# A tuned three-layer cross network on one core: eight 32-row loads near the end, and the first pairs' x-products inside one group of small matmuls

## The chip, the cores and the metric

The kernel runs on one core of one Trainium2 chip. The metric is the device time of the launch in microseconds. A core has a tensor engine (PE, with its weight loads listed as PEld), a vector engine (DVE), a scalar engine (ACT), GpSimd (POOL) and a queue engine (SP) that issues most of the transfers between main memory (HBM) and on-chip memory (SBUF). PE writes into PSUM, a small memory of eight banks of 128 x 512 floats. Each engine runs its own instructions strictly in the order in which they were written; between engines they wait on semaphores.

## The reference, cut to what matters

Three layers cross the input with itself, and the result is one number for each of the 1024 batch rows. `x` has the shape (1024, 64, 16): batch, features, embedding.

```python
for i in range(3):
    z = einsum('bfe,bge->bfge', x0, h)              # every feature of x by every row of h
    y = einsum('oc,bce->boe', Ws[i], z) + bs[i]     # 128 outputs
    x_i, h = (y[:, :64], y[:, 64:]) if i < 2 else (y, y)
    xs.append(x_i)
pooled = sum(concatenate(xs, axis=1), axis=2)
return pooled @ fc_w.T + fc_b
```

All arithmetic is in float32.

## The kernel before, in words

**Tiling.** The batch is cut into 32 chunks of 32 rows, so that a chunk of `x` is a matrix of 64 features by 512 columns (32 rows by 16 embedding places). Only the rows of W0 that feed the next layer are contracted chunk by chunk; everything behind the final `fc` is folded into a few vectors and small matrices at the start. For a chunk the kernel forms blocks `z` (128 x 2048: four 128 x 512 matrices side by side) as an elementwise product of two shifted copies of the chunk, `xa` (128 x 2048) and `xb` (128 x 512, four of them, j = 0 to 3). PE contracts these blocks with `w_all`, 64 output columns at a time, and two such matmuls run side by side in the two halves of the array. Chunks 0, 1, 4 and 5 (pairs 0 and 2) are done plainly in the banks `acc`. From pair 3 on, two chunks are done together, with sums of blocks (`ws`) that save one of eight contractions; their banks are called `alpha`, `beta`, `delta` and `gamma`. There are thirteen such pairs (`NPAIR`, pairs 3 to 15). Chunks 2 and 3 (pair 1) come last and end in the banks `q`.

**The small matmuls.** Three kinds of product have fewer than 128 rows. `along_x` and `v0x` multiply the chunk's 64 rows of x (`xx`, or `xs`, which is the same pair of chunks with its halves exchanged) by the 64 x 64 matrices `v1` and `v0`; the result of `v0x` is the bank `y`, which DVE then multiplies by x (`x_v0x`, line 353) and sums (`sums`, line 356). `far` multiplies 32 rows of `d` by `dq`, `dh` or `dqh`. `d` holds products of features that lie 32 apart: `far_bank` (line 221) copies the loaded rows to PSUM on ACT, `far_product` (line 225) multiplies them on DVE. In the profile all of these matmuls, and the large ones, have line 598, since one helper (`mm`) records them; they are told apart by their tiles. `plain_extras` (line 652) is the group of small matmuls for chunks 0, 1, 4 and 5; `joint_extras` that of two later pairs; `end_extras` (line 1072) the last one.

**What sets the order.** From line 586 on, nothing is issued at once: `at(when, fn, ...)` puts a call on a list, which is sorted by `when` at line 1160 and then issued. One unit of `when` is about one step of two neighbouring matmuls. `T0 = 33` is the start of pair 3's window, `SPAN = 31` the length of a window. A call's place on the list sets its place in the queue of its engine, and the sequence in which scratch blocks (`take`, `used`) and PSUM banks (`bank`) are handed out.

**Scratch and banks.** The blocks `z` come from a list of 14. PSUM banks have roles: `turns["acc"]` holds four, `turns["set"]` two and `turns["y"]` two, each used in rotation. `pair_bank` (line 683) fixes, at the first pair, which of them serve as `even` (two), `three` (three) and `odd` (one). The `y` banks also hold the PSUM copies of `xb` that `second` (line 625) makes on ACT ahead of a DVE product: with two banks in rotation, a copy waits until DVE has read the copy before the last.

**Around the first window.** `weigh` (line 607) multiplies two 128 x 2048 weight blocks on POOL, `add_up` (line 611) sums each on DVE, and `place` (line 616) writes each sum with four small ACT instructions into `v0` (for v = 0) and `v1` (for v = 1). `v0x` for pairs 0 and 2 needs `v0`, `plain_extras` needs `v1`. `factors` (line 340) takes a finished plain chunk out of its bank: an ACT copy (line 344) and one or two DVE products (lines 348, 349, 351). The first two banks of `y` become pair 3's `alpha` and `delta`.

**Near the end.** `load_last_d` (line 199) loads for pair 1 the rows from which `d` is made (`ds`, tile d) and a second factor (`xds`, tile xs). SP then issues `load_turned` (line 186) and `load_xx` (line 182) for the same pair. DVE runs `far_product` for pair 1 directly ahead of `w_hb` of the last of the thirteen pairs (line 778), which takes a bank out that the first matmul of `end_extras` writes again. Each SP transfer uses one of eight semaphores in rotation, so that a transfer's issue waits for the landing of the eighth transfer before it.

Of the kernel before, what the change touches and what calls it, by code (L numbers as in the profile page):

```python
# [45 lines left out]
CB = 32  # L46
N = CB * E
# [6 lines left out]
XR = 128 + NI  # L54
# [15 lines left out]
def cin_kernel(ctx, tc, xra, xrb, wh, w0r, w1h, w2t, wx1, wx0, vec, lin, out):  # L70
# [7 lines left out]
    halves = [slice(0, F), slice(F, 128)]  # L78

    turns = {"acc": [0, 1, 2, 3], "set": [4, 5], "y": [6, 7]}  # L80
# [40 lines left out]
    fcb, fcr = vs[:, 3:4], vs[:, 68:196]  # L121
# [9 lines left out]
    for base in (0, 64, -64):  # L131
        nc.gpsimd.affine_select(
            out=shift, in_=shift, compare_op=ALU.not_equal, fill=1.0, base=base,
# [43 lines left out]
    def pair_tile(kept, name, k):  # L177
        if k not in kept:
            kept[k] = sp.tile([128, N], F32, tag=name, name=f"{name}_{k}")
        return kept[k]  # L180
# [17 lines left out]

    def load_last_d():
        for kept, name, first in ((ds, "d", 32), (xds, "xs", 0)):  # L200
            for h in halves:
                nc.sync.dma_start(
                    out=pair_tile(kept, name, 1)[h],
                    in_=bass.AP(
                        tensor=xra.tensor, offset=(2 * XR + first) * N,
                        ap=[[XR * N, 2], [N, 32], [1, N]],
                    ),
                )

    def copy_x(c):  # L210
# [18 lines left out]
    def far_pair(when, k):  # L229
        at(when - 2.6, far_bank, k)  # L230
        at(when, far_product, k)
# [50 lines left out]
    acc = const_tile("acc", [128, 2, NCH // 2, CB])  # L282
# [147 lines left out]
    for h in range(2):  # L430
        at = slice(32 * h, 32 * h + 32)
# [156 lines left out]
    def at(when, fn, *args, **flags):  # L588
        ops.append((when, len(ops), fn, args, flags))
# [91 lines left out]
    ROLES = {}  # L681

    def pair_bank(p, name):
        if name not in p:
            n = (p["k"] - 3) % 2
            if not ROLES:
                ROLES["even"] = [turns["acc"][m] for m in (0, 1)]
                ROLES["three"] = [turns["acc"][2], *turns["set"]]
                ROLES["odd"] = turns["acc"][3]
            c = (p["k"] - 3) // 2  # L690
            if name == "delta":
                where = ROLES["odd"] if n else ROLES["even"][1]
            elif name == "alpha":
                where = ROLES["three"][c % 3] if n else ROLES["even"][0]
            else:
                where = ROLES["three"][(c + 1 + n) % 3]
            p[name] = bank(f"{name}_{p['k']}", where)
        return p[name]
# [98 lines left out]
    def make_pair(t, p, when, mixed):  # L797
        a, b = p["a"], p["b"]
        for when, c, j, name, uses in (
            (when[0], b, 2, "B22", 5), (when[1], b, 0, None, 0), (when[2], b, 0, "T3", 9),  # L800
            (when[3], a, 0, "X", 5), (when[4], b, 3, "B22", 5), (when[5], b, 1, None, 0),
            (when[6], b, 1, "T3", 9), (when[7], a, 1, "X", 13 if p["k"] > 3 else 5), (when[8], a, 2, "B21", 5),
            (when[9], a, 3, "B21", 5),
        ):
            if name is None:
                at(t + when, w_both, p, j)
                continue
            if name == "B21" and j == 2 and p["k"] == 3:
                at(t + when, w_product, p, c, j, name, uses, engine=nc.gpsimd)
                continue  # L810
            if name != "T3":
                ahead = 3.3 if p["k"] > 4 and name == "B22" and j == 2 else 2.7
                if p["k"] == 3 and name == "X" and j == 1:
                    ahead = 9.1
                at(t + when - ahead, second, c, j)
            at(t + when, w_product, p, c, j, name, uses)
        t2, t1, t4 = ("T2", "X", "T3"), ("T3", "B22", "T2"), ("T2", "T2", "B21")
        for when, j, names in zip(
            mixed, (0, 1, 1, 0, 1, 1, 0), (t2, (*t2, 0, 2), (*t2, 2), t1, t1, t4, t4)
        ):  # L820
            if names == t4 and j and p["k"] % 2:
                at(t + when - 1.5, w_mix, p, j, *names, 0, 2)
                names = (*t4, 2)
            at(t + when, w_mix, p, j, *names)
        at(t + 29, lambda: used(p["B21"][p["k"] % 2 ^ 1]))
# [81 lines left out]
    def load_pair(t, p, b0, a0, b1, a1):  # L907
        a, b = p["a"], p["b"]
        at(t + b0, load_xa, b)
        at(t + b0, load_xb, b, 2, 0)  # L910
        at(t + a0, load_xa, a)
        at(t + a0, load_xb, a, 0)
        at(t + b1, load_xb, b, 3, 1)
        at(t + a1, load_xb, a, 1, 2, 3)
        early = p["k"] > 3
        at(t - 8 if early else t + 1, load_d, p["k"])
        far_pair(t + (6.9 if p["late"] else 17.5), p["k"])
        at(t + 1.1, load_xx, p["k"])


# [31 lines left out]
    for when, c in ((-7, 4), (1, 5)):  # L952
        at(when, copy_x, c)
        at(when, copy_d, c)
    for v, fc, mul, add, put in ((0, fcr[:, 0:64], 4, 16.6, 16.7), (1, fcr[:, 64:128], 5, 20, 20.1)):
        at(mul, weigh, v, fc)
        at(add, add_up, v)
        at(put, place, v, v1 if v else v0, QS if v else 1.0)
# [3 lines left out]
        at(when, product, c, j, engine=nc.gpsimd, uses=NI)  # L962
    for k in (0, 2):
        at(-0.6, new_y, k, "acc")
        at(24.5, x_v0x, k, k // 2)
        at(24.6, sums, k, slice(0, 128), slice(1, 2), slice(0, CB), slice(k // 2, k // 2 + 1))
    for c in (4, 5):
        at(-0.5, new_acc, c)
    contract_all(0, 4, start=True)
# [1 line left out]
        at(16 + t, contract, 5, t // NI, t % NI, True)  # L971
    for k, when in ((0, 6), (2, 12)):
        far_pair(when, k)
    at(24.1, v0x, 0)
    at(24.1, v0x, 2)
    at(29.1, plain_extras)
    for c in (0, 1):
        at(34.5, factors, c)
    at(34.6, sums, 0, slice(0, 128), slice(0, 1))
    for c, when in ((4, 12.7), (5, 21.4)):  # L980
        at(T0 + when, factors, c)
    at(T0 + 29.1, sums, 2, slice(0, 128), slice(0, 1))

# [9 lines left out]
    for n, p in enumerate(pairs):  # L993
        t = T0 + SPAN * n
        q, after = pairs[n - 1], pairs[n + 1] if n + 1 < NPAIR else None
        if n == 0:
            load_pair(t, p, -39.9, -33.3, -39.8, -27)
            make_pair(
                t, p, (-23.4, -20.7, -20.4, -16.5, -17.2, -16.8, -15.8, -7, -13.5, 3),
                (-14, -6.9, -6.8, 7.2, 12.4, 17.6, 15.9),  # L1000
            )
            first_window(
                t, p, after, [[(contract_half, 5, 3, i, h) for i in (1, 2, 3)] for h in range(2)]
            )
        else:
            load_pair(t, p, -34, -28, -27.8, -27.7)
            make_pair(
                t, p, (-21.4, -18.7, -18.4, -15.8, -12.2, -9.5, -6.1, -6.2 if n % 2 else -2, 1.6, 4.2),
                (-5, 1.6, 3.6, 7.2 if n % 2 else 0.2, 12.4, 18.6, 18.5 if n % 2 else 16.9),
            )  # L1010
            (a_leads if n % 2 else o_leads)(t, p, q, after)
            if n % 2:
                end_pair(t, q, (0.7, 21.4, 21.5, 21.3, 36))
            else:
                end_pair(t, q, (0.7, 22.3, 22.4, 9.9, 36))
# [236 lines left out]
```

## Time and profile before

| | |
|---|---|
| median of 3 runs | 442.82 us (441.85 to 443.77) |
| the profiled execution | 442.79 us, of which 440.9 us are the span from its first to its last instruction |
| granted TensorE clock | 1.0 throughout |
| DVE, POOL, ACT busy | 389.2, 378.0, 114.1 us |
| transfers | 102.04 MB, 231 GB/s on average |

The profile is one execution on the chip. A row of the timeline gives start, duration, engine, line, operation and `out<-in` by the program's names without buffer numbers; what stands in brackets is the time in which the engine sat idle before it and what ended that. Each float32 matmul leaves two rows, so that x8 is four matmuls. Where two of them run side by side in the array, both have the same start. A row of the chain of waits names what the end of the program was waiting for at that time. "SPq" is the issue of a transfer, "DMA" its time until landing.

### The profile page before, as it was taken

What the parts mean: (1) busy time and instruction counts of PE and PEld (TensorE: products, weight loads), DVE (VectorE), ACT (ScalarE), POOL (GpSimd) and SP (SyncE); (2) the same over time, 40 slices, a digit from 0 to 9 for tenths busy, and PEclk for the clock granted to TensorE, in tenths of its full rate; (3) what the DMA queues carried; (4) which work ended last, traced back from release to release, by engine and by line L of the source; (5) the groups of instructions that cost most, each with busy time, mean ns of one, the idle gap of its engine ahead of it and who ended that gap; (6) DMA issues with size and microseconds to landing.
All of it is one profiled execution on the core that took longest, in us unless ns stands there. A gap on an engine that the chain in (4) does not pass through costs nothing.

```text
span 440.9 us, 6152 instructions
## 1 busy us (share of the span) xinstructions
PE 435.3 (99%) x2296; PEld 154.9 (35%) x2296; DVE 389.2 (88%) x288; ACT 114.1 (26%) x210; POOL 378.0 (86%) x143
## 2 busy tenths in 40 slices
PE   9999999999999999999999999999999999999987
PEld 6333343334333333333333333333333333333335
DVE  4897799999998999989998989989999889986754
ACT  3153361323311222121322213212221213213111
POOL 5828898899998989899898989989898998989900
PEclk9999999999999999999999999999999999999999
DMA  7997997199649972899729984599818997397400
GB/s 275 411 384 184 352 411 314 46 325 241 224 132 312 325 220 84 229 326 273 247 85 250 341 239 159 155 322 307 225 67 250 335 248 240 119 234 247 113 4 3
DMA packets 36567, 102.04 MB, mean 231 GB/s; under 512 B 6741, under 2 KB 7541, under 8 KB 30073
## 3 DMA queue, kind: packets, MB, share of 16 engines
q1 hardware_dynamic: 33128, 86.84, 58.1%
q0 software_dynamic: 1872, 13.63, 14.9%
q10 hardware_dynamic: 1536, 1.18, 1.0%
q8 instruction: 18, 0.29, 0.3%
q14 instruction: 13, 0.10, 0.1%
HBM read 86.36 MB, written 1.64 MB: 200 GB/s over the span
## 4 chain that ended last, share of the span: by engine, by line
PE 71%; DMA 18%; DVE 6%; issue 3%; SPq 2%; ACT 1%; ACTq 0%; DVEq 0%
PE alpha L598 45%; PE delta L598 20%; DMA xa<-in_xra 6%; DMA xs<-in_xra 4%; DMA z<-in_w2t 3%; PE q L598 2%; DVE z L740 2%; PE acc L598 2%; DVE z L293 2%; DMA xb<-in_xrb 2%; PE y L598 1%; DMA md<-z 1%; DMA z<-md 1%; DMA z<-in_w0r 1%; DVE shift L613 1%
## 5 line engine op out<-in xcount | busy, mean ns | idle before, releaser
L757 POOL TENSOR_TENSOR z<-z,z 128x2048 f32<-128x2048 f32 (+1 forms) x85 | 301.9, 3608 | 21.3 <-PE delta L598 11.1
L740 DVE TENSOR_TENSOR z<-xa,xp 128x2048 f32<-128x2048 f32 x103 | 231.6, 2281 | 10.4 <-ACT xp L627 8.5
L598 PE MATMUL alpha<-z,ws 128*64 128x512 f32 x616 | 228.5, 593 | 0.0
L598 PE MATMUL alpha<-z,w_all 128*64 128x512 f32 x416 | 183.5, 593 | 0.0
L598 PEld LDWEIGHTS alpha<-z,ws 128*64 128x64 f32 x616 | 71.7, 137 | 83.1 <-issue 82.7
L598 PE MATMUL delta<-z,w_all 128*64 128x512 f32 x208 | 95.5, 592 | 0.0
L598 PE MATMUL delta<-z,ws 128*64 128x512 f32 x208 | 91.4, 592 | 0.0
L627 ACT COPY xp<-xb 128x512 f32<-128x512 f32 x88 | 51.1, 587 | 117.6 <-DVE z L740 96.6
L598 PEld LDWEIGHTS alpha<-z,w_all 128*64 128x64 f32 x416 | 56.4, 137 | 58.7 <-issue 58.1
L293 DVE TENSOR_TENSOR z<-xa,xp 128x2048 f32<-128x2048 f32 (+2 forms) x29 | 43.3, 1546 | 8.0 <-ACT xp L627 7.3
L598 PEld LDWEIGHTS delta<-z,ws 128*64 128x64 f32 x208 | 28.4, 137 | 32.5 <-issue 31.7
L598 PEld LDWEIGHTS delta<-z,w_all 128*64 128x64 f32 x208 | 28.4, 137 | 30.9 <-issue 30.5
L293 POOL TENSOR_TENSOR z<-xa,xb 128x2048 f32<-128x2048 f32 x6 | 27.5, 4639 | 10.9 <-DMA xb<-in_xrb 10.9
L598 PE MATMUL acc<-z,w_all 128*64 128x512 f32 x128 | 28.2, 593 | 0.0
L301 PE MATMUL acc<-z,w_all 128*64 128x512 f32 x96 | 21.5, 596 | 0.1
L358 DVE TENSOR_REDUCE acc<-uu 128x64 f32<-128x1024 f32 (+2 forms) x19 | 19.6, 1035 | 0.2
L746 DVE TENSOR_TENSOR xp<-xp,xb 128x512 f32<-128x512 f32 x26 | 18.1, 695 | 0.5
L293 POOL TENSOR_TENSOR z<-xa,xb_gps 128x512 f32<-128x512 f32 (+1 forms) x6 | 14.1, 2376 | 5.2 <-ACT xb_gps L372 4.5
L774 ACT COPY snap<-delta 64x512 f32<-64x512 f32 x13 | 7.6, 581 | 41.1 <-PE alpha L598 36.2
L771 ACT ACTIVATE snap<-alpha,vs 64x512 f32<-64x512 f32 x13 | 8.9, 684 | 35.4 <-PE alpha L598 35.3
L598 PEld LDWEIGHTS acc<-z,w_all 128*64 128x64 f32 x128 | 10.6, 137 | 17.1 <-issue 16.5
L768 ACT COPY alpha<-alpha 64x512 f32<-64x512 f32 x13 | 7.3, 558 | 34.1 <-PE alpha L598 21.0
(137 smaller groups left out, 341.5 us busy)
## 6 DMA issues: line engine op xcount, KB each, us to landing
xa<-in_xra SPq DMA_DIRECT2D x32, 1024.0 KB, 9.0
xb<-in_xrb SPq DMA_DIRECT2D x128, 256.0 KB, 7.8
z<-z POOLq DMA_DIRECT2D x13, 1024.0 KB, 11.3
d<-in_xra SPq DMA_DIRECT2D x28, 128.0 KB, 5.6
xx<-in_xra SPq DMA_DIRECT2D x28, 128.0 KB, 11.5
z<-in_w2t SPq DMA_DIRECT2D x2, 1024.0 KB
z<-in_wx SPq DMA_DIRECT2D x2, 1024.0 KB, 9.8
xs<-in_xra SPq DMA_DIRECT2D x16, 128.0 KB, 6.4
```

What stands on the lines that cost most here:

```text
L293: engine.tensor_tensor(blocks[zs[c, j]][:, at, :], xas[c][:, at, :], xbs[c][j].unsqueeze(1).to_broadcast([128, last - first, N]), ALU.mult,)
L301: nc.tensor.matmul(accs[c][halves[i % 2]], w_all[:, j * NI + i, 0:64], blocks[zs[c, j]][:, i, :], start=(j == 0 and i < 2), stop=(j == las ...
L358: nc.vector.tensor_reduce(acc[rows, of, k, half], uu[rows, of if at is None else at, E * half.start : E * half.stop].rearrange("p k (b e) ...
L598: nc.tensor.matmul(out, w, rhs, start=start, stop=stop, skip_group_check=True)
L613: nc.vector.tensor_reduce(shift[:, 32 * v : 32 * v + 32], w, AX.X, ALU.add)
L627: nc.scalar.copy(out, xbs[c][j])
L740: engine.tensor_tensor(blocks[b], xas[c], xbs[c][j].unsqueeze(1).to_broadcast([128, NI, N]), ALU.mult)
L746: nc.vector.tensor_tensor(bank, bank, xbs[p["b"]][j], ALU.add)
L757: nc.gpsimd.tensor_tensor(*(blocks[b][:, first:last] for b in (o, x, y)), ALU.subtract if in1 == "T3" else ALU.add,)
L768: nc.scalar.copy(beta(p), alpha(p))
L771: nc.scalar.activation(p["t"][p["O"]], alpha(p), AF.Identity, bias=bh1[p["A"]])
L774: nc.scalar.copy(p["hs"][p["A"]], delta(p))
```

## The change

**Eight transfers for four.** `load_last_d` read each half of d and of xs (64 rows) with one transfer whose source pattern has two outer steps (two chunks) of 32 rows. It now issues eight transfers of 32 plain rows, in the order d, d, d, d, xs, xs, xs, xs, all on SP and ahead of the same `load_turned` and `load_xx`.

**The first pairs' x-products.** `v0x` for pairs 0 and 2 moves on the list from 24.1 to 27.1, and `plain_extras` from 29.1 to 27.1, so that the sixteen small matmuls stand together: PE now runs all but one step of chunk 5's plain contraction first, then `v0x` (four matmuls), then `along_x` (four) and `far` (eight), then the one step left, then pair 3's window. `add_up` and `place` for v = 1 move from 20 to 16.7, directly behind those for v = 0. The products of `y` with x (`x_v0x`) go from 24.5 to 27.5, their `sums` from 24.6 to 27.9.

**What gives way.** On DVE the product of pair 3's block for b, j = 1 (tile z, from xp_3) now stands behind the second `add_up` instead of between the two, and the two `sums` of pairs 0 and 2 stand behind pair 3's product "X", j = 1, instead of ahead of it. On ACT the copy for that product "X" stands behind the second `place` instead of ahead of it. `factors` of chunk 4 moves from 12.7 to 15.5 (one DVE product later), pair 3's `far_pair` from 17.5 to 27 (on DVE behind three more 128 x 2048 products, on ACT behind two more copies). `ROLES["three"]` lists the same three banks in another order, so that pair 4's `alpha` takes a bank of chunk 0 instead of one of chunk 4.

No matmul is added or removed, POOL's order is unchanged, and SP has four instructions more.

```diff
     def load_last_d():
         for kept, name, first in ((ds, "d", 32), (xds, "xs", 0)):
-            for h in halves:
+            for m in range(4):
                 nc.sync.dma_start(
-                    out=pair_tile(kept, name, 1)[h],
-                    in_=bass.AP(
-                        tensor=xra.tensor, offset=(2 * XR + first) * N,
-                        ap=[[XR * N, 2], [N, 32], [1, N]],
-                    ),
+                    out=pair_tile(kept, name, 1)[32 * m : 32 * m + 32],
+                    in_=xra[2 + m % 2, first : first + 32],
                 )
...
-                ROLES["three"] = [turns["acc"][2], *turns["set"]]
+                ROLES["three"] = [*turns["set"], turns["acc"][2]]
...
                 if p["k"] == 3 and name == "X" and j == 1:
-                    ahead = 9.1
+                    ahead = 10.9
...
-        far_pair(t + (6.9 if p["late"] else 17.5), p["k"])
+        far_pair(t + (6.9 if p["late"] else 17.5 if early else 27), p["k"])
...
-    for v, fc, mul, add, put in ((0, fcr[:, 0:64], 4, 16.6, 16.7), (1, fcr[:, 64:128], 5, 20, 20.1)):
+    for v, fc, mul, add, put in ((0, fcr[:, 0:64], 4, 16.6, 16.65), (1, fcr[:, 64:128], 5, 16.7, 16.75)):
...
     for k in (0, 2):
         at(-0.6, new_y, k, "acc")
-        at(24.5, x_v0x, k, k // 2)
-        at(24.6, sums, k, slice(0, 128), slice(1, 2), slice(0, CB), slice(k // 2, k // 2 + 1))
+        at(27.5, x_v0x, k, k // 2)
+        at(27.9, sums, k, slice(0, 128), slice(1, 2), slice(0, CB), slice(k // 2, k // 2 + 1))
...
-    at(24.1, v0x, 0)
-    at(24.1, v0x, 2)
-    at(29.1, plain_extras)
+    for k in (0, 2):
+        at(27.1, v0x, k)
+    at(27.1, plain_extras)
...
-    for c, when in ((4, 12.7), (5, 21.4)):
+    for c, when in ((4, 15.5), (5, 21.4)):
...
-                t, p, (-23.4, -20.7, -20.4, -16.5, -17.2, -16.8, -15.8, -7, -13.5, 3),
-                (-14, -6.9, -6.8, 7.2, 12.4, 17.6, 15.9),
+                t, p, (-23.4, -20.7, -20.4, -16.5, -17.2, -16.8, -15.8, -5.2, -13.5, 3),
+                (-14, -5.1, -5, 7.2, 12.4, 17.6, 15.9),
```

## The prediction

> **What bounds the kernel now.** I read the page first, then the waits of PE, then PE's timeline at the two places where PE waits, then the engines that feed these places.
>
> ```profile
> span 440.9 us, 6152 instructions
> PE 435.3 (99%) x2296; PEld 154.9 (35%) x2296; DVE 389.2 (88%) x288; ACT 114.1 (26%) x210; POOL 378.0 (86%) x143
> PE alpha L598 <- DVE snap L778: 1.7, 1, 1.7
> PE y L598 <- ACT v L619: 0.5, 1, 0.5
> ```
>
> PE is busy in 99% of the span, and two of its three waits (the third, 0.8 us, is the start) lie just where the change works: 1.7 us before the last small matmuls, 0.5 us before the first `y`. So time is won here only where PE waits or where its own work gets shorter. In the windows between, the chain of waits shows PE at a fixed pace:
>
> ```profile
> 276.22 0.86 PE y L598 x8
> 327.36 0.86 PE y L598 x8
> ...
> POOL z L757 <- PE delta L598: 11.1, 6, 2.1
> ```
>
> Two pairs take 51.14 us, and POOL, itself busy for 86% of the span, waits for PE there (up to 2.1 us at a time). What PE wins ahead of these windows is therefore kept through them, and what it wins at the end is kept if nothing later in the end is slower.
>
> **The end: what is removed.** The wait of 1.7 us, followed back through the chain, and the DVE and PE rows beside it:
>
> ```profile
> 400.36 19.01 DMA xs<-in_xra
> 419.59 0.69 DVE d L227
> 420.31 0.77 DVE snap L778
> 421.12 0.55 PE alpha L598
> ...
> 411.28 4.48 DVE L293 TENSOR_TENSOR z<-xa,xp 128x2048 f32<-128x2048 f32 x2
> 419.59 0.69 DVE L227 TENSOR_TENSOR d<-d,xs 128x512 f32<-128x512 f32 x1 [3.84 <-DMA xs<-in_xra]
> ...
> 414.72 4.68 PE L598 MATMUL q<-z,w_all 128*64 128x384 f32 x28
> 421.12 0.65 PE L598 MATMUL alpha<-xx,v 64*64 64x512 f32 x2 [1.72 <-DVE snap L778]
> ```
>
> The last of the four transfers of `load_last_d` takes 19.01 us for 128 KB. DVE's `far_product` waits for it 3.84 us, `w_hb` (line 778) is queued behind that product, and PE's first small matmul waits for `w_hb`: 1.72 us. Why so slow: the transfer engines are nearly idle meanwhile.
>
> ```profile
> 402.00:404.00 2.00, 2.00 (x14) 0.58 (x10) 2.00 (x2) 0.20 (x1) 2.00 (x1) 1.00 0.16 55
> 410.00:412.00 2.00, 2.00 (x12) 0.72 (x10) 1.97 (x3) 0.00 (x0) 2.00 (x2) 1.00 0.94 215
> 412.00:414.00 2.00, 2.00 (x12) 0.71 (x10) 2.00 (x2) 0.41 (x1) 2.00 (x1) 1.00 0.21 51
> 416.00:418.00 2.00, 2.00 (x16) 0.92 (x14) 0.00 (x0) 0.00 (x0) 2.00 (x1) 1.00 0.13 51
> ```
>
> The last two columns are the share of the 16 transfer engines and GB/s: 0.13 to 0.16 of 16 is about two engines, at 51 to 55 GB/s. So a transfer with the outer step of two chunks creeps through two engines (128 KB by 51 GB/s is 2.6 us each, 10.3 us for four), and at 410 to 412 us, at a share of 0.94, these two also carry the large copies of POOL. Loads of 64 plain rows of the same tensor (line 194) behave otherwise:
>
> ```profile
> DMA to landing us min/median/max: 2.6/5.6/5.7
> ```
>
> The new transfers are plain rows, so I price their landing by this row, the nearest: at most 5.7 us. The other bound is that a 32-row piece still goes through two engines: 64 KB by 51 GB/s, eight of them, the same 10.3 us. The Trainium skill, "DMA: Bandwidth & Descriptors", section "Why a DMA increments its semaphore by 16 and not by 1", says that a transfer uses the largest number of engines up to 16 that divides the slowest dimension of both sides; that is 2 for the old pattern, 16 for 32 rows. Its 2 agrees with the 0.13 of 16 above; its 16 no row here shows for these loads, so it only lowers the chance of the other bound. By it the sum stays as below; by two engines for the new loads too, it is case (c) of the rivals.
>
> **The end: what is added.** Four more issues on SP, and all that follows them there moves back:
>
> ```profile
> L202 SPq DMA_DIRECT2D xs<-in_xra x2: 629/813/997, 398.2 to 400.4; - x2
> 404.93 1.17 SPq L184 DMA_DIRECT2D xx<-in_xra  x2
> ```
>
> An issue costs 0.63 to 1.0 us, so four cost 2.5 to 4.0 us, and the last `xx` is issued at 408.6 to 410.1 us instead of 406.1. (The last xs now waits for a semaphore of an xb load, but the old program's issues at 401.4 and after had waited for the same ones.) The last xs is issued near 404 us. With 5.7 us, xs lands before 410 and `xx` before 416 us. Their neighbours agree: at 412 to 414 us the share has fallen to 0.21, so that what was then left was the two creeping queues, some 8 us by 2 engines, about 1 us of all 16. DVE's products end at 411.28 + 4.48 = 415.76; then 0.69 for `far_product` and 0.77 for `w_hb` give 417.2 us. PE's q matmuls end at 414.72 + 4.68 = 419.4 us. So PE goes on without a wait, and 1.72 us are won. The cover is 2.2 us on DVE and 3.4 us on the loads; the early gain below takes 1.05 of each if DVE and the loads did not move with PE (they do in part, since SP waits for PE at its `d` loads).
>
> **The first window.** PE before:
>
> ```profile
> 59.43 17.37 PE L598 MATMUL acc<-z,w_all 128*64 128x512 f32 x80
> 77.28 0.89 PE L598 MATMUL y<-xx,v 64*64 64x512 f32 x2 [0.49 <-ACT v L619]
> 78.55 3.65 PE L598 MATMUL acc<-z,w_all 128*64 128x512 f32 x16
> 82.13 0.65 PE L598 MATMUL acc<-xx,v 64*64 64x512 f32 x2
> 83.15 0.64 PE L598 MATMUL acc<-d,dq 32*64 32x512 f32 x1
> 84.19 0.64 PE L598 MATMUL delta<-z,ws 128*64 128x512 f32 x1
> ...
> 121.72 0.65 PE L598 MATMUL alpha<-xx,v 64*64 64x512 f32 x2
> 123.59 0.65 PE L598 MATMUL delta<-d,dh 32*64 32x512 f32 x2
> ```
>
> A matmul's end overlaps its follower by some 0.16 us (an estimate: 0.59 us a row, against a pace of 0.43), so the first row is done at 59.43 + 17.37 - 0.16 = 76.64: 20 steps of two neighbouring matmuls, 0.86 us each. The detour for `y` lasts from there to 78.55, 1.91 us. In the joint event of the next pair, `along_x` and `v0x` together take 123.59 - 121.72 = 1.87 us; `along_x` alone took 83.15 - 82.13 = 1.02 us. Moved into the event, `y` costs 0.85 us: 1.05 us are won, of which 0.49 are the wait for ACT and the rest two changes of the array's layout. The step of chunk 5 put behind the event (two matmuls) keeps its price.
>
> Does the event find its inputs? `y` now starts three steps of 0.86 after 76.64, at 79.2 us, and `along_x` near 80.1.
>
> ```profile
> 74.21 2.28 DVE L613 TENSOR_REDUCE shift<-z 128x32 f32<-128x2048 f32 x1
> 76.41 2.28 DVE L740 TENSOR_TENSOR z<-xa,xp 128x2048 f32<-128x2048 f32 x1
> 80.80 1.40 DVE L354 SCALAR_TENSOR_TENSOR uu<-y,cx,xx 128x512 f32<-128x512 f32 x2
> 83.30 2.28 DVE L740 TENSOR_TENSOR z<-xa,xp 128x2048 f32<-128x2048 f32 x1
> 76.52 0.96 ACT L619 ACTIVATE v<-shift 64x32 f32<-64x32 f32 x4 [6.95 <-DVE shift L613]
> 71.01 4.55 POOL L609 TENSOR_TENSOR z<-z,vs 128x2048 f32<-128x2048 f32 x1 [1.19 <-DMA z<-in_wx]
> 85.72 13.75 POOL L757 TENSOR_TENSOR z<-z,z 128x1024 f32<-128x1024 f32 x4 [1.13 <-DVE z L740]
> ```
>
> The second sum takes the place of the product at 76.41 (POOL's weighing ends at 75.56) and ends at 78.69; ACT's four instructions end 0.96 later, 79.7 us, 0.4 before `along_x`. The displaced product runs 78.6 to 80.9, the two `y` products 80.8 to 82.2: pair 3's `delta` and `alpha` (the same banks) start at 84.2 - 1.05 = 83.15 us, 0.95 later. Product "X" follows at 82.1 instead of 83.30, since the sums (82.2 to 83.30) now stand behind it; its ACT copy waits for the bank of the displaced product (80.9) and is done by 81.5. POOL waits for "X" and so starts 1.1 us earlier, its chain keeping step with PE. The transfer POOL issues behind that chain,
>
> ```profile
> 99.42 0.93 POOL L755 DMA_DIRECT2D z<-z  x1
> 110.85 0.59 PE L598 MATMUL delta<-z,w_all 128*64 128x512 f32 x1
> z<-z POOLq DMA_DIRECT2D x13, 1024.0 KB, 11.3
> ```
>
> lands by its median at 110.7 us, 0.13 ahead of its matmul; it must move with PE, and I take it that it does (1.1 against 1.05). `far_pair` behind three products costs DVE up to 0.7 us of waiting for its copy (the bank comes free only with the product just ahead); behind it in DVE's queue stand the sums of chunks 4 and 5, `w_hb` of pair 3 and the next products. Nobody needs its result before the event at 123.59, so I price it at nothing; without that cover, 0.7 us. The bank order and the later `factors` add no instruction: nothing.
>
> **Sum.** 442.79 - 1.72 - 1.05 = 440.0 us for an execution like the profiled one; that stands 0.03 us from the median of 442.82.
>
> **Rivals.** *(a) The early gain is lost*: the transfer of 11.3 us, or DVE (0.7 us late behind the copy), makes PE wait in pair 3's or 4's window, and only the end's 1.72 remain: 441.1. For it: the 0.13 us; against: POOL issues earlier. Chance 0.17. *(b) The wait at the end is replaced*: the pieces land well but `xx` or DVE's chain is late, so that PE waits for about the 1.05 us it comes earlier and more; if all of 1.72 comes back, 441.7. For it: `xx` is issued 2.5 to 4.0 us later; against: the cover above. Chance 0.10. *(c) Slower: the pieces still creep.* They go through two engines as before, and the last of them is issued 2.5 us later. The last old xs landed at 400.36 + 19.01 = 419.4 us; the new one lands at 421.9, and PE starts its small matmuls at 423.6 instead of 421.12. PE's early gain then only lengthens its wait, except that SP's loads move forward with PE by up to 1.05: 442.79 + 2.5 - 1.05 = 444.2. It decides from the point where the last xs lands later than 419.4 - 0.69 - 0.77 = 417.9 us, when PE begins to wait. The Trainium skill, "DMA: Bandwidth & Descriptors", section "Bandwidth", speaks for it: batch to 1 MiB, transfers under 64 KB are ruled by their descriptors, and here 128 KB become 64. Against: the plain loads' 5.7 us. Chance 0.06. *That the change doesn't do what it says* would be 442.8 (the product ends at 415.76 but something else holds `far_product`): 0.03. The forecast keeps 0.64.
>
> **How the numbers follow.** About 0.5%, 2.2 us, is what a measurement of this kernel can tell from no change, so faster means below 440.6. The forecast lies 0.6 us under that; of its 0.64 I count 0.56 as faster, and little of the rivals: 0.58. Slower by over 0.5% (above 445.0) needs (c) with its upper 4.0 us: 442.79 + 4.0 - 1.05 = 445.7; most of (c) and what I have not seen go there, 0.05. The same: 0.37. The range reaches from 438.9 (both gains, with 1 us of scatter, as the runs of 441.85 to 443.77 have) to 441.8, which takes in (a) and (b).
>
> **What would show it.** Right: PE has neither the wait for line 778 nor that for line 619; the transfer share near 402 and 416 us no longer stays at 0.1 to 0.2; `far_product` starts directly behind DVE's products; the first `delta` matmul of pair 3 starts near 83.1, and two pairs still take 51.14 us. Wrong: any wait of PE before `delta` in the first window or between 100 and 112 us, or one before the end's small matmuls with xs, xx or DVE named.

## The result, and the profile after

| | before | changed |
|---|---|---|
| median of 8 runs each, side by side | 442.3 us (441.82 to 443.77) | 440.12 us (439.69 to 441.39) |
| ratio | | 0.995, 95% interval 0.9935 to 0.9966 |
| profiled execution, its span | 442.79, 440.9 us | 440.44, 438.6 us |

The change gains 2.2 us, 0.5%, just at the bound that the prediction set for telling a change at all; the interval lies below 1. The forecast was 440.0. The page of the changed kernel, and all of PE's waits in it (engine, line and tile; what it waited for; us in total, times, longest):

```profile
span 438.6 us, 6160 instructions
PE 435.1 (99%) x2296; PEld 173.8 (40%) x2296; DVE 388.7 (89%) x288; ACT 114.1 (26%) x210; POOL 377.9 (86%) x143
...
PE misc L127 <- PEq L1238: 0.8, 1, 0.8
```

The waits of 1.7 and 0.5 us are gone; what is left is the start. PE has lost no work, it only waits less. From `load_last_d` on, lines of the changed file are three lower than before (598 is now 595).

**The end.** The timeline of the changed kernel, SP, DVE and PE:

```profile
403.42 1.11 SPq L188 DMA_DIRECT2D xs<-in_xra  x2
404.63 1.72 SPq L184 DMA_DIRECT2D xx<-in_xra  x2
410.50 4.47 DVE L290 TENSOR_TENSOR z<-xa,xp 128x2048 f32<-128x2048 f32 x2
414.89 0.68 DVE L224 TENSOR_TENSOR d<-d,xs 128x512 f32<-128x512 f32 x1
415.61 0.76 DVE L775 SCALAR_TENSOR_TENSOR snap<-alpha,vs,snap 64x512 f32<-64x512 f32 x1
413.87 4.73 PE L595 MATMUL q<-z,w_all 128*64 128x384 f32 x28
418.53 0.65 PE L595 MATMUL alpha<-xx,v 64*64 64x512 f32 x2
```

`far_product` (now line 224) follows DVE's two products at once, with no bracket where 3.84 us stood; the snap ends at 416.37, 2.2 us before PE needs its bank. The last two columns of the windows by 2 us, the share of 16 transfer engines and GB/s, show why:

```profile
402.00:404.00 2.00, 2.00 (x13) 0.79 (x10) 2.00 (x2) 0.59 (x1) 2.00 (x2) 1.00 0.44 106
410.00:412.00 2.00, 2.00 (x12) 0.93 (x10) 2.00 (x2) 0.00 (x0) 2.00 (x1) 1.00 0.62 168
412.00:414.00 2.00, 2.00 (x12) 0.88 (x10) 2.00 (x2) 0.59 (x1) 2.00 (x2) 1.00 0.04 8
416.00:418.00 2.00, 2.00 (x15) 1.12 (x12) 1.58 (x2) 0.00 (x0) 2.00 (x1) 1.00 0.00 0
```

The long tail at 0.13 to 0.16 is gone; from 412 us there is next to nothing left to move.

**The first window, and what follows.** The timeline of the changed kernel, PE, DVE, ACT and POOL:

```profile
25.01 0.23 PE L453 MATMUL pcx<-vs,res 64*64 64x1 f32 x4
78.76 0.65 PE L595 MATMUL y<-xx,v 64*64 64x512 f32 x2
82.59 0.59 PE L595 MATMUL delta<-z,ws 128*64 128x512 f32 x1
99.09 0.61 PE L595 MATMUL alpha<-z,ws 128*64 128x512 f32 x1
119.81 0.65 PE L595 MATMUL alpha<-xx,v 64*64 64x512 f32 x2
171.90 0.65 PE L595 MATMUL alpha<-xx,v 64*64 64x512 f32 x2
107.53 0.69 DVE L224 TENSOR_TENSOR d<-d,xx 128x512 f32<-128x512 f32 x1 [0.66 <-ACT d L220]
98.26 0.69 ACT L768 ACTIVATE snap<-alpha,vs 64x512 f32<-64x512 f32 x1 [1.84 <-PE alpha L595]
84.47 13.78 POOL L754 TENSOR_TENSOR z<-z,z 128x1024 f32<-128x1024 f32 x4
126.23 1.15 POOL L752 DMA_DIRECT2D z<-z  x1
```

And in the kernel before the same first landmark, and three rows that are used further down:

```profile
25.49 0.23 PE L456 MATMUL pcx<-vs,res 64*64 64x1 f32 x4
101.00 0.61 PE L598 MATMUL alpha<-z,ws 128*64 128x512 f32 x1
100.17 0.68 ACT L771 ACTIVATE snap<-alpha,vs 64x512 f32<-64x512 f32 x1
127.55 1.07 POOL L755 DMA_DIRECT2D z<-z  x1
```

Two readings need care. First, this execution was 0.48 us ahead at 25 us (25.01 against 25.49), long before any changed code: that is scatter between executions, and must not be counted for the change. So I measure stretches between landmarks: from there to pair 3's first `delta` it is 57.58 us, before 84.19 - 25.49 = 58.70, so 1.12 us won. Second, the lead doesn't last. The first joint event (the small matmuls `alpha<-xx,v` of pairs 3 and 4) is 1.91 us earlier than before (119.81 against 121.72), the second, two pairs later, only 0.96: the two pairs between took 52.09 us instead of 51.14. The weight loads name the place; the timeline of PEld, a row of the changed kernel, in its bracket the idle time and what ended it:

```profile
140.86 0.13 PEld L595 LDWEIGHTS delta<-z,w_all 128*64 128x64 f32 x1 [0.77 <-DMA z<-z]
```

That is the addition that POOL leaves to a transfer (issued at 126.23). The waits of PE itself list nothing there: the weight load's wait of 0.77 us cost PE 0.95, but it is booked on another row. The landing of this one transfer, in the kernel before and then in the changed one:

```profile
DMA to landing us min/median/max: 13.5/13.5/13.5
```

```profile
DMA to landing us min/median/max: 14.6/14.6/14.6
```

### The profile page after: what moved, and what is told of

It is laid out like the page before. It is cut to its first block, busy times and chain, and to the rows that moved or that the text cites. A ratio compares the mean times of both kernels' runs of the same rounds, so it can differ in the third digit from the quotient of the medians.

```text
span 438.6 us, 6160 instructions
## 1 busy us (share of the span) xinstructions
PE 435.1 (99%) x2296; PEld 173.8 (40%) x2296; DVE 388.7 (89%) x288; ACT 114.1 (26%) x210; POOL 377.9 (86%) x143
## 4 chain that ended last, share of the span: by engine, by line
PE 99%; DVE 0%; issue 0%
PE alpha L595 50%; PE delta L595 24%; PE acc L595 7%; PE acc L298 5%; PE q L595 3%; PE acc L331 3%; PE acc L307 2%; PE y L595 2%; PE xp L268 1%; PE gamma L595 1%; PE misc L127 1%; PE pv L415 0%; PE pm L444 0%; PE po L1023 0%; DVE hb L1173 0%; PE pl L1169 0%
## 5 line engine op out<-in xcount | busy, mean ns | idle before, releaser
L754 POOL TENSOR_TENSOR z<-z,z 128x2048 f32<-128x2048 f32 (+1 forms) x85 | 301.7, 3616 | 20.7 <-PE delta L595 11.3
L595 PEld LDWEIGHTS alpha<-z,ws 128*64 128x64 f32 x616 | 76.3, 137 | 83.1 <-issue 78.2
## 6 DMA issues: line engine op xcount, KB each, us to landing
z<-z POOLq DMA_DIRECT2D x13, 1024.0 KB, 10.8
```

What stands on the lines that cost most here:

```text
L595: nc.tensor.matmul(out, w, rhs, start=start, stop=stop, skip_group_check=True)
L754: nc.gpsimd.tensor_tensor(*(blocks[b][:, first:last] for b in (o, x, y)), ALU.subtract if in1 == "T3" else ALU.add,)
```

## The experiments

For all of them PE's time is cut at the same five landmarks: the `pcx` row near 25 us; pair 3's first `delta`; the first, second and last (sixth) joint event; the small matmuls of the end (the `alpha<-xx,v` row near 420 us). Each figure is the difference of two rows of PE's timeline in the one profiled execution.

| kernel | pcx to delta | to 1st event | 1st to 2nd | 2nd to 6th | 6th to end |
|---|---|---|---|---|---|
| before | 58.70 | 37.53 | 51.14 | 204.55 | 43.71 |
| changed | 57.58 | 37.22 | **52.09** | 204.66 | 41.97 |
| changed, again | 57.64 | 37.25 | **51.38** | 204.56 | 41.92 |
| loads alone | 58.36 | 37.52 | 51.14 | **206.41** | 42.58 |
| event alone | 57.64 | 37.62 | **51.45** | **205.03** | 43.41 |
| eight loads, two steps | 57.53 | 37.26 | **52.47** | 204.55 | 44.33 |
| pair 4's transfer earlier | 57.54 | 37.49 | 51.14 | 204.56 | 42.02 |
| all even pairs' transfers earlier | 57.54 | 37.21 | 51.14 | 204.55 | 41.93 |
| three small edits undone | 57.63 | **38.95** | 51.14 | **205.26** | 42.04 |
| far_pair undone | 57.54 | **38.22** | 51.14 | 204.63 | 41.92 |
| banks and factors undone | 57.59 | 37.22 | 51.14 | 204.55 | 42.06 |
| half of the loads old | 57.63 | 37.22 | **51.59** | 204.55 | 42.08 |
| v placed early, alone | 58.71 | 37.61 | 51.14 | 204.56 | 43.34 |
| all but the event | 57.86 | 37.27 | 51.14 | 204.55 | 41.92 |

Below, times are medians, and ratios are to the kernel before in runs on the same chip, with their 95% interval.

**1. The loads alone.** The kernel before with this edit:

```diff
-            for h in halves:
+            for m in range(4):
                 nc.sync.dma_start(
-                    out=pair_tile(kept, name, 1)[h],
-                    in_=bass.AP(...
+                    out=pair_tile(kept, name, 1)[32 * m : 32 * m + 32],
+                    in_=xra[2 + m % 2, first : first + 32],
                 )
```

> The kernel before with only the eight 32-row loads in place of the four. My theory: the end's 1.72 us come from the pattern of these loads alone, so PE's wait for the snap of the end is gone, DVE's far_product starts directly behind its last two products, and the time is 1.7 us under the kernel before (some 440.6 against 442.3), with the rest of the trace as before. Rival: the loads land in time in the changed kernel only because its event had moved SP's work forward; then a wait of 0.5 to 1.7 us of PE at the end's small matmuls stays here, and the time is 441.1 to 442.3.

440.97 us, ratio 0.9965 (0.9952 to 0.9978): 1.55 us. PE has no wait at the end's small matmuls and `far_product` follows the products at once; the loads need no help from the event. (Its last stretch is 0.6 us longer than in the changed kernel; 0.44 of that is a wait of PE for ACT's snap at 410.29.) The profiled execution itself took 443.67, because it lost 1.9 us between the second and the sixth event. PEld's timeline says where:

```profile
193.94 0.13 PEld L595 LDWEIGHTS delta<-z,w_all 128*64 128x64 f32 x1 [0.83 <-DMA z<-z]
...
348.19 0.13 PEld L595 LDWEIGHTS delta<-z,w_all 128*64 128x64 f32 x1 [0.65 <-DMA z<-z]
```

The same kind of wait, at pairs that the change doesn't touch: these transfers land close to their use all along the kernel.

**2. The event alone.** The changed kernel with the old `load_last_d`.

> The changed kernel with the old four loads put back. My theory: the transfer share of 0.1 to 0.2 of 16 engines is back at the end and PE waits there again, by 1.7 us if SP's loads have moved forward with PE and by up to 2.7 us if they haven't. PE is some 0.9 us ahead of the kernel before from 172 us to the end's q matmuls, so the time is 441.4 to 442.3. Rival: the event's gain holds in full and the wait at the end doesn't grow: 1.05 us under the kernel before, 441.2 or less. Rival: nothing of the event's gain is left: 442.3, and PE's lead at 172 us is 0.

441.94 us, ratio 0.9991 (0.9979 to 1.0002): by itself the event gives 0.4 us, and even that can't be told from nothing. In the profile 1.06 us were won up to pair 3's `delta`; 0.31 were lost between the first two events, 0.48 in the next four; the wait at the end was back at 1.41 us, less than the 1.7 or more that I expected. My theory's range holds the time; "nothing is left" is wrong for the trace.

**3. The old pattern, in eight transfers.** The changed kernel with:

```diff
+            for h in halves:
+                for m in range(2):
+                    nc.sync.dma_start(
+                        out=pair_tile(kept, name, 1)[h, 256 * m : 256 * m + 256],
+                        in_=bass.AP(
+                            tensor=xra.tensor, offset=(2 * XR + first) * N + 256 * m,
+                            ap=[[XR * N, 2], [N, 32], [1, 256]],
```

> The changed kernel, with the loads of the end as eight transfers that keep the old pattern of two outer steps (64 rows by half the columns each; bytes and number as in the changed kernel). My theory, that the pattern sets the number of transfer engines: the share of 0.1 to 0.2 and 50 GB/s are back until 418 us or later, far_product waits for xs, and PE waits 1.7 us or more at the end; 441.8 or more. Rival, that eight small transfers are quicker than four large ones whatever their pattern: no wait of PE at the end, 440.1 as the changed kernel.

443.07 us, ratio 1.0025 (1.0011 to 1.004): about 3 us over the changed kernel (0.995, and 0.9957 when run again). In the profiles the end is 2.36 us of that. Its waits of PE and of DVE, and the windows:

```profile
PE alpha L599 <- DVE snap L779: 1.8, 1, 1.8
...
420.14 0.69 DVE L228 TENSOR_TENSOR d<-d,xs 128x512 f32<-128x512 f32 x1 [3.72 <-DMA xs<-in_xra]
...
402.00:404.00 2.00, 2.00 (x12) 0.65 (x10) 1.61 (x1) 0.88 (x2) 2.00 (x1) 1.00 0.18 61
404.00:406.00 2.00, 2.00 (x12) 0.65 (x10) 2.00 (x2) 0.59 (x1) 2.00 (x3) 1.00 0.14 46
418.00:420.00 2.00, 1.86 (x12) 0.57 (x8) 0.00 (x0) 0.00 (x0) 1.32 (x1) 1.00 0.13 47
```

Same bytes, same number of transfers, and the tail at two engines and about 50 GB/s is back with the whole wait. The rows are half as long as those of the new pieces, but the old loads, with full rows, crept just so. So it is the pattern that decides, not the number. The rule in the Trainium skill, "DMA: Bandwidth & Descriptors", section "Why a DMA increments its semaphore by 16 and not by 1" (a transfer uses the largest number of engines up to 16 that divides the slowest dimension of both sides), agrees: in the tails of the four kernels whose xs loads have two outer steps the share is 0.10 to 0.18 of 16, and 32 plain rows left no such tail.

**4. Pair 4's transfer earlier.** The changed kernel with one number changed, so that POOL issues this transfer ahead of the addition that stood before it:

```diff
-                (-5, 1.6, 3.6, 7.2 if n % 2 else 0.2, 12.4, 18.6, 18.5 if n % 2 else 16.9),
+                (-5, 1.6, 3.6, 7.2 if n % 2 else 0.2, 12.4, 18.4 if n == 1 else 18.6, 18.5 if n % 2 else 16.9),
```

> The changed kernel with pair 4's accumulating transfer issued by POOL one addition earlier (4.6 us, near 121.6 instead of 126.23 us). My theory: in the changed kernel 0.95 us of PE's early lead are lost between 122 and 172 us because the weight loads of pair 4's delta wait 0.77 us for this transfer near 140.9 us. Then that wait is gone here, two pairs take 51.14 us in this stretch too instead of 52.09, and the time is up to 0.9 us under the changed kernel, 439.2 to 439.6. Rival: POOL, which has no idle time between 71 and 131 us, is late with its additions as such; then the addition behind the transfer is later by the transfer's issue, the wait moves to POOL's sums, and the time is as the changed kernel (440.1) or up to 0.5 us longer.

439.97 us, ratio 0.9947 (0.9935 to 0.9959), above the 439.2 to 439.6 that I expected. The transfer's row:

```profile
123.45 0.88 POOL L752 DMA_DIRECT2D z<-z  x1 [0.31 <-POOL z L754]
```

It is issued 3.6 us earlier against PE's first event, not 4.6. No weight load waits for such a transfer any more, and the two pairs take 51.14 us: what was lost there is kept. The time alone, 0.15 us under the changed kernel, doesn't tell the two apart; the trace does.

**5. All even pairs' transfers earlier** (`18.4 if n % 2 else 18.6`), with **6. the changed kernel again** beside it.

> The changed kernel with the accumulating transfer of every even pair (4, 6, 8 and so on) issued one addition earlier, not only pair 4's. My theory: in each of these pairs the transfer lands close to the weight load that needs it, so single executions lose 0.4 to 1.1 us at one pair or another, as the kernel with the loads alone did at 193.94 and 348.19 us. Then no weight load waits for such a transfer by more than 0.3 us in this kernel, PE loses nothing between 122 us and the end, and the median is 0.2 to 0.8 us under the changed kernel (439.3 to 439.9), with the single times closer together. Rival: the waits are rare, and the addition that is issued later costs as much; then 440.1 or more.

> The changed kernel once more, beside the kernel with the earlier transfers. My theory: 440.1 again, and the weight loads of pair 4's delta wait for its transfer near 141 us again by 0.5 to 1.2 us, whatever lead this execution has at 25 us. Rival: that wait was an accident of the first profile, which ran 0.5 us ahead before the changed code began; then there is none here.

439.66 us, ratio 0.9937 (0.9918 to 0.9956), against 440.6, ratio 0.9957 (0.994 to 0.9973), for the changed kernel in the same comparison. That is 0.9 us in the medians and the best kernel of this study; the two intervals still overlap, so its size is open. In the profile with the earlier transfers no weight load waits for such a transfer, PE loses nothing from the first event to the sixth, and the row of the landings of all thirteen such transfers has moved; first the changed kernel's row, then this one's:

```profile
DMA to landing us min/median/max: 8.0/10.8/14.6
```

```profile
DMA to landing us min/median/max: 8.0/9.2/11.3
```

In the changed kernel again the two pairs lost 0.24 us, not the 0.5 to 1.2 that I expected, and no weight load near 141 us is shown waiting by more than 0.2: the place is the same (1st to 2nd event), the size varies from execution to execution. Five profiled executions with the event and the old place of the transfer lost 0.24 to 1.33 us there (changed, again, event alone, eight loads, half of the loads old), one lost nothing (banks and factors undone); the two in which an undone edit had already cost 1.0 us or more lost nothing more there.

**7. The three edits priced at nothing, undone**, and then **far_pair alone** and **banks and factors alone**:

```diff
-                ROLES["three"] = [*turns["set"], turns["acc"][2]]
+                ROLES["three"] = [turns["acc"][2], *turns["set"]]
...
-        far_pair(t + (6.9 if p["late"] else 17.5 if early else 27), p["k"])
+        far_pair(t + (6.9 if p["late"] else 17.5), p["k"])
...
-    for c, when in ((4, 15.5), (5, 21.4)):
+    for c, when in ((4, 12.7), (5, 21.4)):
```

> The changed kernel with the three edits that I priced at nothing undone: the order of the three banks, far_pair of the third pair at its old place, and the factors of chunk 4 at theirs. Expected by the prediction: no change, 440.1 within 0.4 us. Rival: they are needed; with the old order of the banks pair 4's first sums wait for DVE's factors of chunk 4, or far_pair stands ahead of a product and makes it late, so that PE or a weight load waits 0.3 us or more between 84 and 110 us with DVE named: 440.4 to 441.5.

> The changed kernel with far_pair of the third pair back at its old place, the bank order and the factors as changed. My theory, from the kernel with three edits undone: there ACT's snap stood behind a copy that waited for the product behind far_pair, ended at 100.86 us, and PE waited for it. So here PE waits for ACT's snap near 100 us again, loses 0.4 to 0.9 us there, and the time is 440.5 to 441.2. Rival: the factors of chunk 4 alone were late; then no wait here, 440.1 to 440.6.

> The changed kernel with the order of the three banks and the factors of chunk 4 back, far_pair as changed. My theory: the factors stand 0.73 us ahead of a product that PE needs at 99 us, so PE or a weight load waits for DVE's product there by 0.3 to 0.6 us, and the time is 440.4 to 440.9; the order of the banks has no wait of its own. Rival: nothing waits, 440.1 to 440.4, and the whole loss of the three edits was far_pair's.

All three undone: 441.66 us, ratio 0.9982 (0.997 to 0.9993). `far_pair` alone: 440.68, ratio 0.9966 (0.9948 to 0.9983). Banks and factors alone: 440.48, ratio 0.9954 (0.9938 to 0.997), and nothing waits, against what I expected of the factors (the time lies in the range that I gave for a wait; the trace shows none). The stretch from pair 3's `delta` to the first event is 1.73, 1.00 and 0.00 us longer than in the changed kernel. The timeline with all three undone, PE, ACT and DVE:

```profile
99.64 1.04 PE L595 MATMUL alpha<-z,w_all 128*64 128x512 f32 x2 [0.38 <-DVE z L737]
101.01 0.62 PE L595 MATMUL alpha<-z,ws 128*64 128x512 f32 x1 [0.33 <-ACT snap L768]
99.57 0.59 ACT L624 COPY xp<-xb 128x512 f32<-128x512 f32 x1 [2.30 <-DVE z L737]
100.18 0.68 ACT L768 ACTIVATE snap<-alpha,vs 64x512 f32<-64x512 f32 x1
96.56 0.73 DVE L348 SCALAR_TENSOR_TENSOR uu<-acc,vs,snap 64x512 f32<-64x512 f32 x1
97.22 2.27 DVE L737 TENSOR_TENSOR z<-xa,xp 128x2048 f32<-128x2048 f32 x1
99.42 0.68 DVE L224 TENSOR_TENSOR d<-d,xx 128x512 f32<-128x512 f32 x1
```

Both waits of PE come out of DVE's queue. The factors (line 348, 0.73 us) stand ahead of a product, which ends at 99.49 and is late for PE at 99.64; and ACT's snap stands behind a copy which can only start when that product has freed its bank, so the snap ends at 100.86 and PE starts at 101.01. `far_pair` adds to both: its copy on ACT takes one of the two banks in rotation, so that the next copy must wait for one product more. With it out of the way the snap doesn't queue there: in the changed kernel it ran at 98.26. Undone alone, the factors fit.

The brackets show only 0.71 of the 1.73 us. The whole loss is in the start of the first `alpha<-z,ws` behind the snap: counted from pair 3's `delta`, it comes at 16.50 us in the changed kernel, at 18.23 with all three undone, at 17.50 with `far_pair` undone and at 16.50 with banks and factors undone, which is 1.73, 1.00 and 0.00 later. Until then PE runs on with the matmuls of the other half of the array, so that most of the delay is not listed as a wait of PE. In the kernel before, where all three stood as here, the same row comes at 16.81 (101.00 - 84.19) behind a snap that ends at 100.85. That is 0.31 us later than in the changed kernel, all of the 0.31 by which its stretch is longer. So these edits also won something there, though not in every execution: in "all but the event", with the same old order, the row comes at 16.55. (Pair 4's transfer earlier and event alone lost 0.27 and 0.40 us in this stretch in another way: a weight load waited some 1 us for an addition of POOL.)

**8. Half of the loads old**: d by the two old transfers, xs by the four new ones.

> The changed kernel with the two loads of d by the old pattern of two outer steps, and the four 32-row loads of xs kept. My theory: two creeping transfers at 2.6 us each are done some 8 us before far_product needs them, so the wait of PE at the end stays away (440.1), though the share of 16 engines shows 0.1 to 0.2 for some us after the copies. Rival: the two engines that d creeps through also carry a sixteenth of each xs piece, so xs lands late too, and PE waits up to 1.7 us: 440.6 to 441.8.

439.96 us, ratio 0.9946 (0.993 to 0.9962), no wait of PE at the end. Changing the two xs loads alone would have been enough. The share is 0.18 at 412 to 414 us and 0.03 after: two creeping transfers fit into the time, four did not.

**9. v placed early, alone**: the kernel before with

```diff
-    for v, fc, mul, add, put in ((0, fcr[:, 0:64], 4, 16.6, 16.7), (1, fcr[:, 64:128], 5, 20, 20.1)):
+    for v, fc, mul, add, put in ((0, fcr[:, 0:64], 4, 16.6, 16.65), (1, fcr[:, 64:128], 5, 16.7, 16.75)):
```

> The kernel before with one part of the event's change alone: the sum and the place of the second v ahead of a product, as in the changed kernel, while y keeps its detour ahead of the event. By my working of the event, 1.05 us, of which 0.49 are PE's wait for ACT and 0.56 two changes of the array's layout: PE's wait for ACT's v is gone here, the detour takes 1.4 us instead of 1.9, PE is 0.5 us ahead of the kernel before at 85 us, and the time is at most 0.5 us under it. Rival: the wait for ACT was the whole gain; then PE is 1.0 us ahead here. Rival: the displaced product makes PE or a weight load wait later; then nothing is left by 122 us.

442.49 us, ratio 1.0012 (0.9993 to 1.0032), and PE still waits 0.5 us for ACT ahead of `y`. My expectation misread the kernel: `y` needs `v0`, which this edit doesn't move; `v1` is for `along_x`. What remains of it: the displaced product costs nothing.

**10. All but the event**: the kernel before with the new loads and the earlier transfers.

> The kernel before with the eight 32-row loads and the earlier accumulating transfers of the even pairs, but without the event and its edits. My theory: the event is worth 1.05 us once no transfer takes it back, so this kernel is 1.05 us over the kernel with all three (439.66 before now), 440.5 to 440.9, and PE's wait of some 0.5 us for ACT's v is there. Rival: the earlier transfers were all of that kernel's gain over the changed one, and the event gives nothing; then 439.7 here too.

440.83 us, ratio 0.9961 (0.9945 to 0.9977). The event with its edits is the one difference to the best kernel, 1.1 us by the ratios (0.0024 of 442.2), which is what the working had; but the intervals overlap, and the profiled execution shows how loosely that figure sits. It took 439.88 us, and its detour for `y` was cheap:

```profile
75.01 0.96 ACT L616 ACTIVATE v<-shift 64x32 f32<-64x32 f32 x4 [5.55 <-DVE shift L610]
...
76.43 0.65 PE L595 MATMUL y<-xx,v 64*64 64x512 f32 x2
```

Here `v0` was done at 75.97, before PE wanted it, and from `pcx` to `delta` it took 57.86 us: 0.32 over the best kernel. In the profiled execution of the kernel before, with ACT late (76.52 + 0.96), it was 1.16 over it. Of this difference, 0.49 is PE's wait and 0.25 lies in `y`'s own matmuls, which take from 77.28 to 78.55 there and from 76.43 to 77.45 here.

## Why the prediction was right, and where it wasn't

**The end: right, 1.74 us for 1.72.** From the sixth event to the end's small matmuls it is 43.71 us before and 41.97 after. In all ten executions with the new xs loads it is 41.92 to 42.58, in the four without 43.34 to 44.33. Experiments 1 and 3 show that it is the loads' pattern, by itself.

**The added issues: mis-sized, without effect.** Four more issues were to cost SP 2.5 to 4.0 us. The rows of line 202 in the changed kernel (durations in ns, min/median/max), and of line 188 before:

```profile
L202 SPq DMA_DIRECT2D d<-in_xra x4: 311/367/412, 396.5 to 399.6; - x4
L202 SPq DMA_DIRECT2D xs<-in_xra x4: 310/311/311, 400.3 to 403.1; - x4
```

```profile
L188 SPq DMA_DIRECT2D xs<-in_xra x2: 596/1692/2787, 401.4 to 404.2; - x2
```

A plain piece takes 0.31 to 0.41 us to issue, half of what a two-step load took. And one of the issues behind them had stood for 2.79 us before; now the pair of them takes 1.11. So both `xx` are issued by 406.35 us (404.63 + 1.72), not by 408.6 to 410.1; before, it was 406.1. The row I took was that of the pattern being removed; the row of line 194, which the prediction used for the landing, has 0.47:

```profile
L194 SPq DMA_DIRECT2D d<-in_xra x26: 465/472/645, 84.3 to 381.0; - x26
```

**The event: right in its sum, wrong in its parts.** 1.12 us against 1.05. But the 0.49 us of waiting and 0.56 of layout changes were not the parts: with ACT in time the detour cost 0.32 us in all (experiment 10), so some 0.8 hung on `v0`'s being late, well over the 0.49 that PE's row shows as waiting. The event's worth is 0.3 to 1.2 us, by whether ACT is in time.

**The step that failed: "it must move with PE, and I take it that it does".** The prediction looked at pair 3's transfer, which moved by 1.28 us (99.42 to 98.14) and made one weight load wait 0.24 us. It didn't look at pair 4's, which fell behind: it moved by 1.32 us (127.55 to 126.23) while PE's first event moved by 1.91. POOL could not come earlier: in the kernel before its chain began at 85.72 after 1.13 us of idleness, in the changed one at 84.47 with none. So "what PE wins ahead of these windows is kept through them" held only behind the second event, and the sign that two pairs still take 51.14 us failed with 52.09. This is rival (a), at its second place and in part: of the lead, 0.95 us went here in the first profiled execution, 0.24 in the second. Experiments 4 and 5 show the cause: the transfer moved, the loss gone.

The lag of 0.59 us is only part of it. Counted from the first event, pair 4's transfer is issued and lands like this (us; the landing is its row in each trace):

| kernel | issued | time to land | landed | lost, 1st to 2nd event |
|---|---|---|---|---|
| before | 5.83 | 13.5 | 19.3 | 0 |
| changed | 6.42 | 14.6 | 21.0 | 0.95 |
| changed, again | 6.78 | 13.5 | 20.3 | 0.24 |
| event alone | 6.79 | 13.6 | 20.4 | 0.31 |
| eight loads, two steps | 6.81 | 14.6 | 21.4 | 1.33 |
| half of the loads old | 6.47 | 14.0 | 20.5 | 0.45 |
| banks and factors undone | 6.16 | 13.3 | 19.5 | 0 |
| pair 4's transfer earlier | 2.83 | 8.8 | 11.6 | 0 |

What lands later than about 20.1 us is lost, to within 0.1 us in every row. The kernel before had some 0.8 us to spare. In the first profile of the changed kernel the issue fell back by 0.59 and the landing took 1.1 us longer; in the second the issue alone, 0.95 later, used the room up. The prediction's 11.3 us hid this: in the kernel before, the odd pairs' transfers land in 10.4 to 11.3 us, the even pairs' in 13.3 to 13.6, and the median of all thirteen says nothing of pair 4's.

**Why the time still came out at 440.1.** The profiled difference of 2.35 us adds up as 0.48 (scatter ahead of the change) + 1.12 (event) + 0.31 (to the first event) - 0.95 (pair 4) - 0.11 (to the sixth) + 1.74 (end) = 2.59, less 0.24 behind the last landmark. The loss at pair 4 was covered by 0.79 us that don't belong to the event's working: 0.48 of scatter, and 0.31 that the edits priced at nothing won in this execution. The level fits by chance too: the forecast took 2.77 us off 442.79, and the measured gain is 2.2 off a kernel before that stood at 442.3 in the comparison. So the forecast fits partly by luck.

**The edits priced at nothing: right that they cost nothing, incomplete in what they are.** The changed kernel's `far_product` waits 0.66 us at 107.53, as predicted, and no one minds. But moving `far_pair` is not idle: without it 1.00 us goes before the first event, with the factors undone too 1.73. These edits make the room for an earlier PE, and the 0.31 us to the first event are won by them (experiment 7). The prediction priced what they add and not what they clear.

**The rivals.** (b), a new wait at the end, and (c), pieces that still creep, didn't happen; (c) is what experiment 3 built, and it came out at 443.07, against the 444.2 that the prediction gave it. The rule cited for (c), to batch into large transfers (the Trainium skill, "DMA: Bandwidth & Descriptors", section "Bandwidth"), didn't decide here: the 64 KB pieces landed in time where 128 KB ones crept, and 64 KB ones crept too with the old pattern.

## What to carry to other kernels

When one engine is brought forward by a microsecond, list everything that must arrive earlier with it, through two or three windows and not only the next, and ask of each whether its own engine has idle time to follow: one that has none sets the new pace. Measure between landmarks rather than from the start, and look at the weight loads' waits beside those of the matmuls. For a late transfer, look at how many transfer engines it uses before its size or number.

## What was not expected of the hardware

A load of 32 plain rows takes 0.31 us to issue, one of 64 plain rows 0.47 (the median of line 194). With two outer steps of 32 rows it was 0.50 to 1.21 us for the xs loads (before, event alone, v placed early) and 0.57 to 1.78 in experiment 3. How much of that is the pattern and how much the creeping transfers already under way is not separated: a plain load of 64 rows right behind them stood for 2.79 us.

In the changed kernel an accumulating transfer of 1 MB took 13.3 to 14.6 us to land in the even pairs and 8.0 to 10.8 in the odd ones. Issued 3.4 to 4.2 us earlier against PE (experiment 5), those of the even pairs not only had more time but landed sooner, in 8.4 to 9.2 us. Why is open.
